# A four-layer graph network on one core: layer entries turned by VectorE and DMAs instead of TensorE, and dense block transposes

## The chip, the core and the metric

The kernel runs on one core of one Trainium2 chip. The core has five engines with an instruction queue each: TensorE (PE; its weight loads stand as PEld), VectorE (DVE), ScalarE (ACT), GpSimd (POOL) and SyncE (SP). SP issues all of this kernel's DMAs. SBUF is the working memory of 128 partitions, PSUM takes what TensorE computes, and DRAM holds inputs, outputs and scratch. The engines run beside each other and are held together by semaphores; each takes its own instructions in the order in which they stand.

The metric is the device time of one execution in microseconds (us), the median over several runs. A profile of one execution shows, in addition, when every instruction started and what it waited for.

## The reference

`x` holds 32 graphs of 512 nodes with 128 features, `adj` is a 512x512 matrix of zeros and ones. Four layers follow each other. Each normalizes x over the features, cuts it at zero, computes something of it and adds that to x:

```python
# before each layer: h = max(layernorm(x), 0);  x = x + layer(h)
# layer 0: attention over adj
x_h  = elu(h @ Wi + bi)
e    = sigmoid(a_tgt[:, :, None] + a_src[:, None, :] + be[0]) * mask(adj)
recv = elu(concat([e @ x_h, x_h * e.sum(-1, keepdims=True)]) @ Wn + bn)
out  = concat([recv, x_h]) @ Wm + bm
# layer 1: a gated step, five times
m  = adj @ h;  av = concat([m, m]);  u3 = h @ u3_w.T + u3_b
z  = sigmoid(av @ w3_w.T + w3_b + u3)
r  = sigmoid(av @ w4_w.T + w4_b + u3)
hv = tanh(av @ w5_w.T + w5_b + (r * h @ u5_w.T + u5_b))
h  = (1 - z) * h + z * hv
# layer 2: adj @ (h @ weight) + bias
# layer 3: h, adj h, adj^2 h, adj^3 h, each times its own 128x128 weight, summed
```

Results are float32.

## The kernel before

**Two layouts.** A graph stands in SBUF either by nodes (a node's number on the partition, four chunks of 128 nodes side by side, each with its 128 features along the row) or by features (a feature on each partition, the 512 nodes along the row). A product with a weight needs the features on the partitions, the product with adj needs the nodes there, and the layernorm needs the nodes there too. So each graph changes its layout at the entry of layers 0, 1 and 3, and after each of the five steps of layer 1.

**From nodes to features** goes over TensorE: `transposed` (L324) makes four 128x128 transposes into a PSUM bank, and `copied` (L350) has ACT copy the bank to SBUF. Layer 0 does this at L457, layer 1 at L696, the entry of layer 3 at L807.

**From features back to nodes** goes over VectorE and two DMAs: `turned` (L333), called at the end of each step of layer 1 (L729). VectorE transposes blocks of 32x32 (L337), and reads its source with a step of four elements while it does. A DMA writes the result to a scratch buffer `m` in DRAM (L340), and a second DMA reads it back in another order of partitions (L342). The result is in nodes, its features in an order that `by_chunk` undoes where ACT and VectorE read it (`parts`, L665, or `add_to_x`, L370).

**Adjacency.** `A_r` holds adj transposed, as float32r. Since adj has only zeros and ones, the branch taken splits the other operand in two float32r parts (`parts`: ACT makes the high one at L672, VectorE the low one at L675) and multiplies in eight passes (`times_adj`, L680). The program holds a second branch for other adjacencies, which doesn't run here.

**The order.** Nothing in the code above issues instructions at once. Each call adds an operation to a plan (`Plan.op`, L53), with its engine, an assumed duration, an assumed time until its result is known (`result`, for DMAs that until landing), a due time, and the buffers it takes. `Plan.order` (L98) then runs through time, and whenever an engine is free gives it, of the operations that are ready, the one with the earliest due time. What comes out is a fixed order for every engine; on the chip each engine follows it and waits where data is late. 32 graphs pass through in groups of four (G = 4), with several graphs in different layers at the same time; due times are spaced by PACE = 56 us for each graph.

**Buffers.** The kinds that matter here are `f` (36 tiles of 128x512 float32 in SBUF), `m` (8 scratch tiles in DRAM), `b` (the 8 banks of PSUM), and `d` (4 rows of DRAM).

**The gather.** For each graph from the fifth on, layer 0 brings a column of scores into a row by two DMAs: `d<-s` (L488) writes 512 single numbers to DRAM, and `f<-d` (L502) reads the row back to all partitions.

Of the kernel before, what the change touches and what calls it, by code (L numbers as in the profile page):

```python
# [16 lines left out]
P = 128  # L17
# [21 lines left out]
class Plan:  # L39
# [13 lines left out]
    def op(self, eng, us, due, emit, reads=(), writes=(), two=False, keep=0, result=None):  # L53

        o = Op(eng, us, self.RESULT[eng] if result is None else result, emit, two, keep)
        for v in reads:
            o.before.add(v.writer)  # L60
        for v in writes:
            o.before.update(v.readers)
            if v.writer:
                o.before.add(v.writer)
            elif v.kind and v.slot is None:
                o.takes.append(v)
        for v in reads:
            v.readers.append(o)
        for v in writes:
            v.writer, v.readers = o, []  # L70
        o.vals = [v.whole or v for v in dict.fromkeys([*reads, *writes])]
        for v in o.vals:
            v.left += 1
        for v in [*reads, *writes, *o.vals]:
            self.vals[v] = True
        o.before -= {o, None}
        o.due = max([due, *(b.due for b in o.before)])
        for b in o.before:
            b.after.append(o)
        self.ops.append(o)  # L80
# [100 lines left out]
def tile_four_graph_layers(  # L181
# [27 lines left out]
    nc = tc.nc  # L209
    B, N, D = x.shape  # L210
    NC = N // P
    G = 4
# [7 lines left out]
    T_MM, T_TR, T_NARROW, T_PASS = 0.86, 0.44, 0.224, 0.23  # L220
    T_VEC, T_COPY, T_ACT = 0.61, 0.5, 0.6
# [3 lines left out]
    op = plan.op  # L225
# [19 lines left out]
    def at(v):  # L245
        if v.tile is not None:
            return v.tile
        return places[v.kind][v.slot] if v.whole is None else at(v.whole)[:, v.part]
# [28 lines left out]
    def load_const(src, shape, name, due, us=0.5):  # L277
        return load(const(name, shape), src, due, us)

    def load_column(src, name, due):  # L280
        return load_const(src.rearrange("(p o) -> p o", o=1), [P, 1], name, due, 0.4)
# [13 lines left out]
    Wi_sb = load_const(Wi, [P, P], "Wi_sb", -9)  # L295
# [3 lines left out]
    bi_sb = load_column(bi, "bi_sb", -8)  # L299
# [20 lines left out]
    bi_half, bn_half = scaled(bi_sb, 0.5, "bi_half", 6), scaled(bn_sb, 0.5, "bn_half", 8)  # L320
# [3 lines left out]
    def transposed(src, due):  # L324

        pt = Val("b")
        def emit():
            for c in range(NC):
                nc.tensor.transpose(at(pt)[:, ts(c, P)], at(src)[:, ts(c, P)], at(ident))  # L329
        op("PE", T_TR, due, emit, [src, ident], [pt])  # L330
        return pt

    def turned(src, due):  # L333


        blocks, moved, t = Val("f"), Val("m"), Val("f")
        op("DVE", 1.03, due, lambda: nc.vector.transpose(  # L337
            at(blocks).rearrange("p (q c f) -> p q c f", c=NC, f=32),
            at(src).rearrange("p (c i q) -> p q c i", c=NC, q=4)), [src], [blocks])
        op("SP", 1.0, due, lambda: nc.sync.dma_start(at(moved), at(blocks)),  # L340
           [blocks], [moved], result=4.0)
        op("SP", 1.0, due, lambda: nc.sync.dma_start(  # L342
            at(t).rearrange("p (b e) -> p b e", e=P),
            at(moved).rearrange("(b i) (q e) -> (i q) b e", i=32, e=P)), [moved], [t], result=6.0)
        return t

    def by_chunk(t):
        return t.rearrange("p (b c f) -> p c b f", c=NC, f=32)

    def copied(src, due, us=T_COPY):  # L350
        t = Val("f")
        op("ACT", us, due, lambda: nc.scalar.copy(at(t), at(src)), [src], [t])  # L352
        return t

    def product(w, src, due, dst=None, start=True, stop=True):
        dst = dst or Val("b")
        op("PE", T_MM, due, lambda: nc.tensor.matmul(  # L357
            at(dst), at(w), at(src), start=start, stop=stop), [src, w], [dst])
        return dst

    def tanh(dst, src, due, bias, scale=0.5, us=T_ACT):
# [50 lines left out]
    for jc in range(NC):  # L412
        pt, z, odd = Val("b"), Val("f"), Val("f")
# [26 lines left out]
    def elu(p, bias, half, due, keep, scale=1.0):  # L440


        e, t, r = Val("f"), Val("f"), Val("f")
        op("ACT", T_ACT, due, lambda: nc.scalar.activation(
            at(e), at(p), AF.Exp, bias=at(bias), scale=scale), [p, bias], [e], keep=keep)
        tanh(t, p, due, half, scale / 2)
        op("ACT", T_ACT, due, lambda: nc.scalar.activation(
            at(r), at(p), AF.Relu, bias=at(bias), scale=scale), [p, bias], [r])
        op("DVE", T_VEC, due, lambda: nc.vector.scalar_tensor_tensor(
            at(t), at(e), 1.0, at(t), op0=ALU.add, op1=ALU.mult), [e, t], [t], two=True)  # L450
        op("DVE", T_VEC, due, lambda: nc.vector.scalar_tensor_tensor(
            at(r), at(t), 0.0, at(r), op0=ALU.min, op1=ALU.add), [t, r], [r], two=True)
        return r

    def layer0(b, h, due):
        KEEP = 12
        hT = copied(transposed(h, due), due)  # L457
        d = due + 6
        xhT = elu(product(Wi_sb, hT, d), bi_sb, bi_half, d, KEEP)

        d = due + 14
        msg, ends = Val("f"), Val("s")
        for half in range(2):
            pt = Val("b")
# [19 lines left out]
        d = due + 20  # L484
# [20 lines left out]
        for jc in range(NC):  # L505
            e = Val("f")
# [15 lines left out]
        d = due + 30  # L522
# [24 lines left out]
        d = due + 44  # L547
# [41 lines left out]
    def list_rest(exact, pool):  # L589
# [41 lines left out]
        for half in range(2):  # L631
            t, outs = Val("f"), slice(half * P // 2, (half + 1) * P // 2)
            load(t, l3_w[:, outs, :].rearrange("i o k -> i (o k)"), 110, 1.3,
                 to=lambda t: t[:, : P // 2 * K])
# [12 lines left out]
        if exact:  # L647
            adjT = A_r
        else:
            adjT = Val(tile=pool.tile([P, NC, N], F32, tag="AT", name="AT"))  # L650
# [3 lines left out]
            for jc in range(NC):  # L654
                pt = Val("b")
# [21 lines left out]
                [src, hi], [lo], two=two)  # L677
            return [lo, hi]

        def times_adj(tok, due):  # L680

            pa = Val("b")
            def emit():
                for jc in range(NC):
                    for n, part in enumerate(tok):
                        nc.tensor.matmul(  # L686
                            at(pa), at(part)[:, ts(jc, P)], at(adjT)[:, jc, :],
                            start=jc == n == 0, stop=jc == NC - 1 and n == PARTS - 1,
                        )
            op("PE", NC * PARTS * T_ADJ, due, emit, [*tok, adjT], [pa])  # L690
            return pa


        def layer1(b, h, due, pace):
            tok = parts(h, due, two=True)
            h = copied(transposed(h, due), due)  # L696
            for t in range(STEPS):
                d = due + t * pace
                u = copied(product(u3T, h, d), d)
                m = copied(times_adj(tok, d), d)  # L700

                def gate(wT, bias, d, m=m, u=u):
                    pg, s = product(wT, m, d), Val("f")
                    op("DVE", T_VEC, d, lambda: nc.vector.tensor_tensor(  # L704
                        at(s), at(u), at(pg), op=ALU.add), [u, pg], [s])
                    tanh(s, s, d, bias)
                    return s

                d += 3
                rh = gate(w4T, w4b, d)  # L710
                op("DVE", T_VEC, d, lambda rh=rh, h=h: nc.vector.scalar_tensor_tensor(  # L711
                    at(rh), at(rh), 1.0, at(h), op0=ALU.add, op1=ALU.mult),
                    [rh, h], [rh], two=True)
                z = gate(w3T, w3b, d + 1)
                d += 4
                pc = product(w5T, m, d, stop=False)
                product(u5T, rh, d, pc, start=False)
                c = Val("f")
                tanh(c, pc, d, w5b, 1.0)

                op("DVE", T_VEC, d, lambda c=c, h=h: nc.vector.tensor_tensor(  # L721
                    at(c), at(c), at(h), op=ALU.subtract), [c, h], [c], two=True)
                op("DVE", T_VEC, d, lambda c=c, z=z: nc.vector.scalar_tensor_tensor(  # L723
                    at(c), at(z), 1.0, at(c), op0=ALU.add, op1=ALU.mult), [z, c], [c], two=True)
                op("DVE", T_VEC, d, lambda c=c, h=h: nc.vector.scalar_tensor_tensor(
                    at(c), at(c), 0.5, at(h), op0=ALU.mult, op1=ALU.add), [c, h], [c], two=True)
                h = c
                d += 5
                h_tok = turned(h, d)  # L729
                if t + 1 < STEPS:  # L730
                    tok = parts(h_tok, d + 9, True, by_chunk)
                else:
                    add_to_x(b, h_tok, d + 9, by_chunk, True)
# [61 lines left out]
        for g in range(NG):  # L795
            bs = range(g * G, (g + 1) * G)
            hT = []
            for b in bs:
# [3 lines left out]
                t = begin(b) + (2.0 if G <= b < B - G - 1 else 1.2) * PACE  # L802
# [49 lines left out]
```

## Time and profile before

| | us |
|---|---|
| median of three runs (1743.92 to 1748.58) | 1746.67 |
| the profiled execution | 1748.12 |
| its span, first to last instruction | 1746.3 |
| mean clock granted to TensorE, of full speed | 0.994 |

The costliest groups that the change touches or stands beside, from the profile (line, operation, count, busy time, mean of one):

| group | count | busy us | mean ns |
|---|---|---|---|
| L686 matmul with adj, 128x512, float32r (layers 1 and 2) | 1536 | 427.6 | 421 |
| L357 matmuls with layer 1's weights, five of them | 1600 | 818.1 | 592 to 599 |
| L329 transposes on TensorE | 384 | 57.6 | 277 |
| L352 copies PSUM to SBUF on ACT | 448 | 256.5 | 588 |
| L337 block transposes on VectorE | 160 | 176.5 | 1105 |
| L704 adds of the gates on VectorE | 320 | 213.6 | 679 |

To read it: a group is all instructions of one line, engine, operation and shape. An fp32 matmul of 512 columns shows as two records, so L357 has 1600 for 800 products. [...] the next begins before it ends, so its mean isn't what the stream of matmuls advances by. Idle time of an engine before a group is named with what ended it. The time of a DMA is counted from its issue on SP to its landing.

### The profile page before, as it was taken

How to read it: one execution, taken by the hardware profiler on the slowest of the kernel's cores; microseconds unless marked ns; L12 is line 12 of the kernel's file. 1: busy time of each engine (PE TensorE's matmuls, PEld its weight loads, DVE VectorE, ACT ScalarE, POOL GpSimd, SP SyncE). 2: the span in 40 equal slices, each digit the busy share in tenths (PEclk: the TensorE clock that was granted, in tenths of full speed). 3: DMA queues.
4: the chain of work that ended last, by engine and by line, in shares of the span. 5: the costliest groups of instructions: out<-in, count | busy, mean ns of one | idle time of the engine just before them, and what ended most of it. 6: DMA issues, size and time to landing. Idle time of an engine off the chain costs nothing.

```text
span 1746.3 us, 21006 instructions
## 1 busy us (share of the span) xinstructions
PE 1695.5 (97%) x6829; PEld 1098.0 (63%) x6829; DVE 1479.3 (85%) x3213; ACT 1135.2 (65%) x2155; POOL 399.8 (23%) x312
## 2 busy tenths in 40 slices
PE   5899999999999999999999999999999999999998
PEld 3555555566666666665666666666666656656797
DVE  6899999999898887888888898888899879878752
ACT  6767765778666666665765667666768656655451
POOL 4521210332222211222212221122232212001110
PEclk9999999999999999999999999999999999999999
DMA  4022322322222222223221221222322131221201
GB/s 109 7 53 75 85 73 73 81 52 85 52 58 61 79 67 46 74 75 55 67 55 60 79 61 61 67 52 81 67 67 55 50 84 61 73 72 58 76 13 48
DMA packets 164534, 112.07 MB, mean 64 GB/s; under 512 B 23232, under 2 KB 139840, under 8 KB 164416
## 3 DMA queue, kind: packets, MB, share of 16 engines
q1 hardware_dynamic: 164416, 110.65, 23.9%
q8 instruction: 55, 0.90, 0.3%
q14 instruction: 63, 0.52, 0.2%
HBM read 60.23 MB, written 50.39 MB: 63 GB/s over the span
## 4 chain that ended last, share of the span: by engine, by line
PE 76%; DVE 13%; DMA 4%; ACT 3%; issue 2%; SPq 0%; DVEq 0%; ACTq 0%
PE b L357 33%; PE b L686 17%; PE b L769 9%; PE b L760 6%; DMA f<-m 4%; PE b L525 4%; PE b L552 3%; DVE f L510 2%; PE b L329 2%; DVE f L704 2%; PE b L743 2%; PE b L469 1%; DVE f L337 1%; DVE f L723 1%; DVE r L675 1%
## 5 line engine op out<-in xcount | busy, mean ns | idle before, releaser
L686 PE MATMUL b<-A_r,r 128*128 128x512 f32 x1536 | 427.6, 421 | 4.3 <-DVE r L675 4.2
L352 ACT COPY f<-b 128x512 f32<-128x512 f32 x448 | 256.5, 588 | 210.6 <-PE b L686 119.2
L686 PEld LDWEIGHTS b<-A_r,r 128*128 128x128 f32 x1536 | 287.2, 189 | 109.6 <-issue 38.9
L391 POOL TENSOR_TENSOR s<-s,nhalf 128x4 f32<-128x4 f32 x128 | 156.2, 1221 | 735.9 <-DVE s L389 707.8
L769 PE MATMUL b<-r,A_r 128*128 128x512 f32 x768 | 306.3, 499 | 0.0
L704 DVE TENSOR_TENSOR f<-f,b 128x512 f32<-128x512 f32 x320 | 213.6, 679 | 56.5 <-PE b L357 54.0
L399 ACT ACTIVATE f<-x,s 128x128 f32<-128x128 f32 x512 | 209.9, 488 | 22.3 <-DVE s L394 22.2
L769 PEld LDWEIGHTS b<-r,A_r 128*128 128x128 f32 x768 | 140.6, 189 | 102.6 <-issue 91.5
L516 POOL TENSOR_TENSOR f<-f,f 128x512 f32<-128x512 f32 x96 | 154.1, 1608 | 207.4 <-DVE f L510 131.1
L362 ACT ACTIVATE f<-f,b4w 128x512 f32<-128x512 f32 x160 | 115.8, 724 | 127.3 <-DVE f L704 126.6
L337 DVE STREAM_TRANSPOSE f<-f 128x512 f32<-128x512 f32 x160 | 176.5, 1105 | 0.3
L675 DVE TENSOR_TENSOR r<-f,r 128x512 fp32r<-128x512 f32 x192 | 141.3, 739 | 37.1 <-ACT r L672 37.0
L357 PE MATMUL b<-f,u5T 128*128 128x512 f32 x320 | 163.2, 595 | 8.7 <-DVE f L711 8.7
L357 PE MATMUL b<-f,w4T 128*128 128x512 f32 x320 | 165.2, 599 | 4.1 <-ACT f L352 4.0
L357 PE MATMUL b<-f,w3T 128*128 128x512 f32 x320 | 163.8, 594 | 0.0
L357 PE MATMUL b<-f,w5T 128*128 128x512 f32 x320 | 163.2, 595 | 0.0
L357 PE MATMUL b<-f,u3T 128*128 128x512 f32 x320 | 162.7, 592 | 0.0
L721 DVE TENSOR_TENSOR f<-f,f 128x512 f32<-128x512 f32 x160 | 121.5, 761 | 39.3 <-ACT f L362 39.1
L760 PEld LDWEIGHTS b<-V,f 128*128 128x128 f32 x1024 | 131.7, 191 | 31.1 <-issue 25.1
L362 ACT ACTIVATE f<-b,b5w 128x512 f32<-128x512 f32 x160 | 109.7, 688 | 60.4 <-PE b L357 60.2
L362 ACT ACTIVATE f<-f,b3w 128x512 f32<-128x512 f32 x160 | 115.0, 721 | 50.8 <-DVE f L704 50.5
L525 PE MATMUL b<-f,f 128*128 128x512 f32 x256 | 130.9, 596 | 3.2 <-issue 3.0
(95 smaller groups left out, 2489.9 us busy)
## 6 DMA issues: line engine op xcount, KB each, us to landing
m<-f SPq DMA_DIRECT2D x160, 256.0 KB, 2.0
f<-m SPq DMA_DIRECT2D x160, 256.0 KB, 2.8
x<-in_x_dram SPq DMA_DIRECT2D x32, 256.0 KB, 4.5
out_dram<-x SPq DMA_DIRECT2D x32, 256.0 KB, 2.4
f<-d SPq DMA_DIRECT2D x28, 256.0 KB, 4.1
f<-in_adj_dram SPq DMA_DIRECT2D x4, 256.0 KB, 4.6
f<-in_L_gnn_weight_dram SPq DMA_DIRECT2D x2, 224.0 KB, 2.6
d<-s SPq DMA_DIRECT2D x28, 2.0 KB, 9.1
```

Of the source, the lines that this page charges most:

```text
L337: op("DVE", 1.03, due, lambda: nc.vector.transpose(at(blocks).rearrange("p (q c f) -> p q c f", c=NC, f=32), at(src).rearrange("p (c i q) ...
L352: op("ACT", us, due, lambda: nc.scalar.copy(at(t), at(src)), [src], [t])
L357: op("PE", T_MM, due, lambda: nc.tensor.matmul(at(dst), at(w), at(src), start=start, stop=stop), [src, w], [dst])
L362: op("ACT", us, due, lambda: nc.scalar.activation(at(dst), at(src), AF.Tanh, bias=at(bias), scale=scale), [src, bias], [dst])
L391: op("POOL", 1.2, due, lambda: nc.gpsimd.tensor_tensor(stat(SCALE), stat(VAR), at(neg_half), op=ALU.pow), [s, neg_half], [s])
L399: nc.scalar.activation(at(h)[:, ts(c, P)], at(X[b])[:, c, :], AF.Relu, bias=stat(SHIFT)[:, c : c + 1], scale=stat(SCALE)[:, c : c + 1],)
L525: op("PE", T_MM, d, lambda jc=jc: nc.tensor.matmul(at(pn), at(msg)[:, ts(jc, P)], at(es[jc]), start=jc == 0, stop=False), [msg, es[jc]], [pn])
L675: op("DVE", T_VEC, due, lambda: nc.vector.tensor_tensor(part(lo), whole(), part(hi).bitcast(F32), op=ALU.subtract), [src, hi], [lo], two=two)
L686: nc.tensor.matmul(at(pa), at(part)[:, ts(jc, P)], at(adjT)[:, jc, :], start=jc == n == 0, stop=jc == NC - 1 and n == PARTS - 1,)
L704: op("DVE", T_VEC, d, lambda: nc.vector.tensor_tensor(at(s), at(u), at(pg), op=ALU.add), [u, pg], [s])
L760: nc.tensor.matmul(at(pz)[:, ts(i, D)], at(hT[i])[:, ts(ic, P)], at(V[k]), start=i == 0, stop=last and i == G - 1,)
L769: nc.tensor.matmul(at(pz), at(adjT)[:, jc, ts(ic, P)], at(part), start=False, stop=jc == NC - 1 and n == PARTS - 1,)
```

## The change

It has three parts.

1. `turned` transposes densely: VectorE reads and writes whole rows in order. The write to scratch is as before. [...] the second DMA becomes four, each of 32 partitions. The plan's assumptions change with it: 0.63 us for VectorE (1.03 before), 3.0 us until the write has landed (4.0), 1.6 us for the four issues (1.0 for one), 4.0 us until they have landed (6.0).
2. Since the block transposes are dense, layer 1 keeps its columns in block order: the row of a feature holds, for each of the four quarters of a chunk, the 32 nodes of each chunk. `times_adj` reads adj's columns in that order in layer 1 (`by_block`: 16 runs of 32 elements). Products with weights, gates and sums don't see the order.
3. A new function `turned_back` goes from nodes to features without TensorE: a block transpose on VectorE, four DMAs to scratch, one DMA back. Layer 0 uses it for the graphs from the fifth on (28), layer 1 from the ninth on (24); the first graphs keep TensorE's transposes, with layer 1's copy on ACT putting the columns in block order. In layer 0 the product with Wi reads the block order and writes its PSUM bank in the usual one. Where it is used, the due times of what follows are 8 us later.

```diff
     def turned(src, due):
         blocks, moved, t = Val("f"), Val("m"), Val("f")
-        op("DVE", 1.03, due, lambda: nc.vector.transpose(
-            at(blocks).rearrange("p (q c f) -> p q c f", c=NC, f=32),
-            at(src).rearrange("p (c i q) -> p q c i", c=NC, q=4)), [src], [blocks])
+        op("DVE", 0.63, due, lambda: nc.vector.transpose(at(blocks), at(src)), [src], [blocks])
         op("SP", 1.0, due, lambda: nc.sync.dma_start(at(moved), at(blocks)),
-           [blocks], [moved], result=4.0)
-        op("SP", 1.0, due, lambda: nc.sync.dma_start(
-            at(t).rearrange("p (b e) -> p b e", e=P),
-            at(moved).rearrange("(b i) (q e) -> (i q) b e", i=32, e=P)), [moved], [t], result=6.0)
+           [blocks], [moved], result=3.0)
+        def carry():
+            for q in range(4):
+                nc.sync.dma_start(
+                    at(t)[ts(q, 32), :].rearrange("p (b e) -> p b e", e=P),
+                    at(moved)[:, ts(q, P)].rearrange("(b i) e -> i b e", i=32),
+                )
+        op("SP", 1.6, due, carry, [moved], [t], result=4.0)
         return t
+
+    def turned_back(src, due):
+        blocks, moved, t = Val("f"), Val("m"), Val("f")
+        op("DVE", 0.63, due, lambda: nc.vector.transpose(
+            at(blocks).rearrange("p (b c i) -> p b c i", c=NC, i=32),
+            at(src).rearrange("p (c b f) -> p b c f", c=NC, f=32)), [src], [blocks])
+        def carry():
+            for q in range(4):
+                nc.sync.dma_start(
+                    at(moved)[:, ts(q, P)].rearrange("(b f) e -> f b e", f=32),
+                    at(blocks)[ts(q, 32), :].rearrange("p (b e) -> p b e", e=P),
+                )
+        op("SP", 1.6, due, carry, [blocks], [moved], result=3.0)
+        op("SP", 1.0, due, lambda: nc.sync.dma_start(at(t), at(moved)),
+           [moved], [t], result=4.0)
+        return t
+
+    def by_block(t):
+        return t.rearrange("p (c q i) -> p q c i", c=NC, i=32)
...
-    def product(w, src, due, dst=None, start=True, stop=True):
+    def product(w, src, due, dst=None, start=True, stop=True, view=None):
         dst = dst or Val("b")
-        op("PE", T_MM, due, lambda: nc.tensor.matmul(
-            at(dst), at(w), at(src), start=start, stop=stop), [src, w], [dst])
+        def emit():
+            to = at(dst) if view is None else view(at(dst))
+            of = at(src) if view is None else at(src).rearrange("p (q c i) -> p q c i", c=NC, i=32)
+            nc.tensor.matmul(to, at(w), of, start=start, stop=stop)
+        op("PE", T_MM, due, emit, [src, w], [dst])
         return dst
...
     def layer0(b, h, due):
         KEEP = 12
-        hT = copied(transposed(h, due), due)
+        if b < G:
+            hT = copied(transposed(h, due), due)
+        else:
+            hT = turned_back(h, due)
+            due += 8
         d = due + 6
-        xhT = elu(product(Wi_sb, hT, d), bi_sb, bi_half, d, KEEP)
+        xhT = elu(product(Wi_sb, hT, d, view=by_block if b >= G else None),
+                  bi_sb, bi_half, d, KEEP)
...
-        def times_adj(tok, due):
+        def times_adj(tok, due, view=lambda t: t):
...
-                            at(pa), at(part)[:, ts(jc, P)], at(adjT)[:, jc, :],
+                            at(pa), at(part)[:, ts(jc, P)], view(at(adjT)[:, jc, :]),
...
         def layer1(b, h, due, pace):
             tok = parts(h, due, two=True)
-            h = copied(transposed(h, due), due)
+            if b < 2 * G:
+                pt, h = transposed(h, due), Val("f")
+                op("ACT", T_COPY, due, lambda h=h, pt=pt: nc.scalar.copy(
+                    at(h).rearrange("p (q c i) -> p q c i", c=NC, i=32), by_block(at(pt))),
+                    [pt], [h])
+            else:
+                h = turned_back(h, due)
+                due += 8
             for t in range(STEPS):
                 d = due + t * pace
                 u = copied(product(u3T, h, d), d)
-                m = copied(times_adj(tok, d), d)
+                m = copied(times_adj(tok, d, by_block), d)
```

## The prediction

> **What bounds the kernel now.** I read the page's busy shares first, then the busy time of the long middle stretch, then the pace of TensorE in the chain of waits.
>
> ```profile
> PE 1695.5 (97%) x6829; PEld 1098.0 (63%) x6829; DVE 1479.3 (85%) x3213; ACT 1135.2 (65%) x2155; POOL 399.8 (23%) x312
> ...
> PE 76%; DVE 13%; DMA 4%; ACT 3%; issue 2%; SPq 0%; DVEq 0%; ACTq 0%
> ...
> 100.00:1600.00 1500.00, 1478.02 (x5740) 936.41 (x5739) 1320.23 (x2800) 1002.00 (x1888) 329.27 (x240) 1.00 0.25 66
> ```
>
> PE is busy 97% of the span and 1478 of the 1500 us from 100 to 1600 us, at full clock. Ends of matmuls are modelled, so I check the pace. The chain and the timeline hold unbroken runs:
>
> ```profile
> 131.94 6.87 PE b L357 x16
> ...
> 139.68 3.65 PE b L686 x16
> ...
> 1691.38 5.36 PE b L760 x48
> ...
> 387.82 0.49 PE L329 MATMUL b<-ident,f 128*128 128x128 f32 x3
> ```
>
> One record of an fp32 matmul over 512 columns takes 6.87/16 = 0.429 us (two records a matmul), one of float32r 3.65/16 = 0.228, one 128 wide 5.36/48 = 0.112. Three transposes last 0.49 us, the last of them 0.273 (its own duration in the trace), so one costs the stream (0.49 - 0.273)/2 = 0.109. With the counts of the groups: 1992 x 0.4285 + 2360 x 0.228 + 2048 x 0.111 + 421 x 0.109 = 1665 us. That is what PE needs with no stall. The span is 1746.3, so 81 us are stalls: from the start times of the matmuls 30 lie in the first 100 us, 43 between 100 and 1640 us, 8 at the end. In most stretches of 50 us PE loses 0.2 to 0.3 us: this kernel is bound by PE's stream, and anything taken off PE counts whole unless it comes back as a stall.
>
> **Where the 43 us come from.** The views by line of the DMA issues, and the timeline around 304 us:
>
> ```profile
> m<-f SPq DMA_DIRECT2D x160, 256.0 KB, 2.0
> f<-m SPq DMA_DIRECT2D x160, 256.0 KB, 2.8
> d<-s SPq DMA_DIRECT2D x28, 2.0 KB, 9.1
> ...
> DMA to landing us min/median/max: 2.5/2.8/12.2
> ...
> 303.59 0.37 SPq L488 DMA_DIRECT2D d<-s  x1
> 304.07 0.45 SPq L342 DMA_DIRECT2D f<-m  x1
> 304.56 0.51 SPq L290 DMA_DIRECT2D x<-in_x_dram  x1
> ...
> 315.77 0.62 ACT L672 CAST r<-f 128x512 fp32r<-128x512 f32 x1 [3.53 <-DMA f<-m]
> ...
> 317.17 2.99 PE L686 MATMUL b<-A_r,r 128*128 128x512 f32 x8 [2.11 <-DVE r L675]
> ...
> ACT r L672 <- DMA f<-m: 23.0, 8, 3.7
> ```
>
> The gather d<-s (2 KB in 4-byte pieces, once for each of 28 graphs) takes 9 us, and every DMA issued behind it lands only some 12 us after its issue. A read f<-m that follows it takes 11.5 to 12.2 us instead of 2.8 (fourth line: its longest). ACT waits 3.5 us for it and PE 2.1 us after that. This happened 8 times, 23 us of ACT waits. PE's loss in the 20 us after the gathers sums to 19 us; the other 24 us stand mostly before u5T products that wait for DVE.
>
> [...]
>
> **The change part by part.**
>
> *Entries off PE.* Layer 0 of 28 graphs and layer 1 of 24 lose four transposes each: 52 x 4 x 0.109 = 22.7 us of PE stream. ACT loses the copy behind them: 52, and 8 remain under another line, so 52 x 0.588 = 30.6 us on an engine at 65%; worth nothing by itself.
>
> *VectorE.* A dense transpose: [...] the add of L704 shows 679[...] I take 0.69. Turns save 160 x (1.105 - 0.69) = 66 us, entries add 52 x 0.69 = 36 [...]. Net -30 of 1479. It relieves the waits for u5T; I take 8 of the 24 us, bounds 0 and 15.
>
> *Matmuls over strided columns.* 1280 float32r matmuls read adjT in 16 runs of 128 bytes. [...] I take 0; the upper bound, one lost cycle a run, an estimate of 16 x 0.43 ns (from 0.228 us for 512 columns, 0.45 ns each) x 1280 = 9 us. The 28 Wi products write PSUM in runs of 32: 28 x 0.86 = 24 us in all, taken as unchanged, +5 at most.
>
> *The queue.* A turn goes from 2 DMAs to 5, an entry adds 5: SP issues 160 x 3 + 52 x 5 = 740 more, beside some 460 now. Issues follow each other at 0.48 us (303.59, 304.07, 304.56), so SP's issuing rises by 355 us; it has room for that, but a read now has its last quarter issued 1.5 us after its first, so 4.3 us to landing instead of 2.8. In the program's order of instructions SP also waits, before each DMA, for the one eight places earlier (eight completion semaphores in turn): eight places are now 1.6 turns, not four.
>
> *The planner's margins.* The order on every engine is fixed by the plan, and its costs changed. A turn, from VectorE's start to the landing, was planned at 1.03+0.5+1+4+1+6 = 13.5 us and takes 1.1+2.0+2.8 = 5.9; it becomes 0.63+0.5+1+3+1.6+4 = 10.7 planned and 0.69+2.0+4.3 = 7.0 real. The margin shrinks from 7.6 to 3.7 us. That cover is what hides most gathers now. In PE's order the work that stands between a turn's last product and the matmuls that use it shrinks too: counted from the order with the durations above, median 29.7 to 27.8 us, least 21.3 to 19.2.
>
> *The sum.* In SP's order the first turn DMA behind a gather is a read in 11 of 28 cases before and in 15 after, a write in 7 and in 9 (the rest are entries or loads). Before, the 11 reads cost 19 us, 1.7 each; behind a write nothing was lost. After, a read's plan ends 1.4 us earlier (5.6 against 7.0), its fourth piece is the last in line, and ACT's wait passes to PE nearly one to one: 1.7 + 1.4 to 2.4, so 15 x 3.1 to 4.1 = 46 to 61 us. A turn whose write hits was planned at 12 us for both DMAs, now 9.6, and takes longer (two transfers, 10 + 4.3): about 1.5 us late at PE, 9 x 1.5 = 13 us. Middle: 53 + 13 = 66 against 19, +47; but two hits behind one gather share a stall, so I take +41 (bounds +10, if the cushions of PE's order hold, and +60). Entries behind a gather: their products are for graphs not due yet, 0.
>
> 1746.3 - 22.7 - 8 + 41 = 1756.6 us span; the profiled execution took 1748.1 with its start and end, and the median of the runs is 1746.7, on the span. Forecast 1757.
>
> **Rivals.**
> - *The saving holds (faster, 1726).* One mechanism: the cushion in PE's order, 19 us of work at least against some 12 us of real turn. Seven of the eleven reads behind gathers cost PE nothing before; if a lateness of 1.5 us more stays inside that cushion, stalls stay near 19 us and 1746.7 - 22.7 + 2 = 1726. It decides at an extra gather stall of 22.7 + 8 = 31 us, about 1.2 us a gather. For it: PE's pace, which leaves nothing else to lose. Against: where ACT waited for the DMA, PE waited too.
> - *Balance (1746).* Extra stalls of 25 to 36 us, the lower end of my estimate: within 5 us of now, so within 0.3%, about what a measurement of this kernel can tell from no change.
> - *TensorE or SP pays (slower, 1770).* The strided reads cost 10% (1280 x 23 ns = 29 us), with half of the stalls: 1746.7 - 30.7 + 20 + 29 = 1765, or SP becomes late in bursts of twelve issues (12 x 0.48 = 5.8 us), which adds the 3.7 us margin to some ten turns: 1757 + 20 = 1777. [...] SP's waits of 859 us for DVE (it is mostly idle) against the second.
> - *It does not do what it says:* not possible for the transposes; the order of PE has 104 of 6951 rows less over both branches, and the count agrees.
>
> **Numbers.** My forecast 0.47 (own range 1750 to 1775), the saving holds 0.31, balance 0.13, TensorE or SP 0.09. Slower by over 0.3% 0.57, within 0.3% 0.12, faster 0.31. The range reaches to 1724 on the side of the rival and to 1780: 2 in 10 outside.
>
> **What would show it.** Right: PE's transposes 176 instead of 384 records at L329; the dense transpose near 0.69 us; ACT's wait for f<-m well over 23 us; PE's stalls after gathers two to three times 19 us. Wrong: waits of ACT for DMAs at 23 us or less with PE at the same pace, then 1726; or the spacing of float32r records in layer 1 above 0.228, then the third rival.

## The result, and the profile after

The changed kernel takes 1766.55 us (median of 4 runs) against 1746.46 us before (4 runs): a ratio of 1.0117, 95% interval 1.0095 to 1.0139. It is slower. Its profiled execution has a span of 1764.2 us, 17.9 more than before.

The page of the changed kernel, busy shares, chain and two groups:

```profile
PE 1691.9 (96%) x6621; PEld 1083.7 (61%) x6621; DVE 1449.3 (82%) x3265; ACT 1110.0 (63%) x2103; POOL 400.4 (23%) x312
...
PE 69%; DVE 13%; DMA 10%; ACT 4%; issue 2%; SPq 1%; DVEq 0%; ACTq 0%
...
L704 ACT CAST r<-f 128x512 fp32r<-128x512 f32 x192 | 118.0, 620 | 74.7 <-DMA f<-m 66.4
...
f<-m SPq DMA_DIRECT2D x640, 64.0 KB, 2.0
f<-m SPq DMA_DIRECT2D x52, 256.0 KB, 2.8
```

PE has 208 matmul records fewer (6829 to 6621, the transposes), but its busy time hardly falls and its share does: the work went, the time didn't. In the chain DMA went from 4% to 10%. The cast on ACT (L704, once L672) was idle before it for 23.2 us; now for 74.7, of which 66.4 wait for reads f<-m.

The reads by line, L343, in the changed kernel:

```profile
DMA to landing us min/median/max: 1.7/2.0/11.3
```

And its timeline from 807 us (start, duration, engine, instruction; in brackets the idle time before it and what ended it):

```profile
807.05 0.37 SPq L520 DMA_DIRECT2D d<-s  x1
807.52 1.87 SPq L343 DMA_DIRECT2D f<-m  x4
...
819.11 0.62 ACT L704 CAST r<-f 128x512 fp32r<-128x512 f32 x1 [4.95 <-DMA f<-m]
...
816.92 1.02 PE L384 MATMUL b<-f,u3T 128*128 128x512 f32 x2
821.80 2.07 PE L384 MATMUL b<-f,w4T 128*128 128x512 f32 x2 [3.85 <-ACT f L376]
```

A quarter of a read lands 2.0 us after its issue in the middle, and 11.3 at worst. The timeline is the picture of before at 304 us, deeper: a gather, four reads right behind it, ACT waits 4.95 us for the last of them, and PE then stands for 3.85 us, because the copy it needs is queued on ACT behind that cast.

PE's stalls, worked out as in the prediction (time between matmul starts less the pace of 0.4285, 0.228, 0.111 or 0.109 us a record):

| us of PE | before | after |
|---|---|---|
| stream without stalls | 1665.8 | 1643.1 |
| stalls to 100 us | 24.1 | 30.1 |
| stalls from 100 to 1640 us, within 4 to 24 us of a gather's issue | 19.0 | 55.6 |
| stalls from 100 to 1640 us, elsewhere | 23.7 | 22.8 |

The stream is counts times pace, so its fall says only that 208 records went. By this account 22.7 us of stream were saved and 36.6 given back behind gathers; 6 more came in the first 100 us.

Not all of a stall is standing. The two lines of PE above show it: two records take 1.02 us before the stall of 3.85 us and 2.07 after it. The stretch before 821 us and the one behind it (length, busy time of each engine, then the clock granted to TensorE, third from the end):

```profile
814.00:821.00 7.00, 3.95 (x24) 2.90 (x22) 1.24 (x3) 2.05 (x6) 0.04 (x1) 1.00 0.05 12
821.00:827.80 6.80, 6.00 (x8) 2.80 (x9) 6.80 (x16) 2.95 (x6) 0.00 (x0) 0.50 0.41 136
```

From 100 to 1640 us the trace has seven such stretches at half the clock, 3.4 or 6.8 us long, 30.7 us in all; before it has four, 13.7 us. Each lies at a stall of about 2 us or more, though not every such stall has one. Matmuls that start in them cost some 13 us more than their pace, before 6; these are part of the 78.4 and 42.7 us of stalls between 100 and 1640 us.

### The profile page after: what moved, and what is told of

Same layout as the page of the kernel before. It is cut to its first block, busy times and chain, and to the rows that moved or that the text cites. A ratio compares the mean times of both kernels' runs of the same rounds, so it can differ in the third digit from the quotient of the medians.

```text
span 1764.2 us, 22081 instructions
## 1 busy us (share of the span) xinstructions
PE 1691.9 (96%) x6621; PEld 1083.7 (61%) x6621; DVE 1449.3 (82%) x3265; ACT 1110.0 (63%) x2103; POOL 400.4 (23%) x312
## 4 chain that ended last, share of the span: by engine, by line
PE 69%; DVE 13%; DMA 10%; ACT 4%; issue 2%; SPq 1%; DVEq 0%; ACTq 0%
PE b L384 31%; PE b L718 14%; PE b L808 8%; DMA f<-m 8%; PE b L799 5%; PE b L557 4%; PE b L584 2%; DVE f L542 2%; DMA m<-f 1%; DVE f L743 1%; PE b L782 1%; DVE r L707 1%; PE b L501 1%; DVE s L413 1%; SPq L343 1%
## 5 line engine op out<-in xcount | busy, mean ns | idle before, releaser
L718 PE MATMUL b<-A_r,r 128*128 128x512 f32 x1536 | 434.3, 425 | 2.6 <-DVE r L707 2.6
L376 ACT COPY f<-b 128x512 f32<-128x512 f32 x388 | 223.2, 586 | 191.8 <-PE b L718 119.7
L808 PE MATMUL b<-r,A_r 128*128 128x512 f32 x768 | 321.3, 518 | 0.0
L707 DVE TENSOR_TENSOR r<-f,r 128x512 fp32r<-128x512 f32 x192 | 136.0, 713 | 71.6 <-ACT r L704 60.4
L704 ACT CAST r<-f 128x512 fp32r<-128x512 f32 x192 | 118.0, 620 | 74.7 <-DMA f<-m 66.4
L760 DVE TENSOR_TENSOR f<-f,f 128x512 f32<-128x512 f32 x160 | 116.5, 730 | 29.4 <-ACT f L389 29.1
```

The costliest lines, as they stand in the source:

```text
L707: op("DVE", T_VEC, due, lambda: nc.vector.tensor_tensor(part(lo), whole(), part(hi).bitcast(F32), op=ALU.subtract), [src, hi], [lo], two=two)
L718: nc.tensor.matmul(at(pa), at(part)[:, ts(jc, P)], view(at(adjT)[:, jc, :]), start=jc == n == 0, stop=jc == NC - 1 and n == PARTS - 1,)
L808: nc.tensor.matmul(at(pz), at(adjT)[:, jc, ts(ic, P)], at(part), start=False, stop=jc == NC - 1 and n == PARTS - 1,)
```

## The experiments

Theory A: the plan's shorter assumed times place a turn's consumers closer to their DMAs, so that a DMA held up by a gather, once covered, now stops ACT and then PE. Theory B: the additional DMAs themselves (four reads for one, SP's longer queue) make the turns late. Theory C, beside A: the loss comes from standing behind the gather in SP's queue. The kernel before took 1746 us beside the changed kernel, 1754 beside e1 to e4 and 1759 to 1760 beside the others (e1 to e4 ran on one chip, e5 and e8 to e10 on a second, the rest on a third; why the times differ stays open). So each ratio is to runs of the kernel before that were taken beside it; its stalls and waits are those of its one profile, of 1748 us, and are compared less closely. "Behind gathers" is, as above, what begins within 4 to 24 us of a gather's issue.

| kernel | ratio to before | 95% interval | PE stalls, 100 to 1640 us | of these behind gathers | ACT's cast waits for f<-m, us (times) |
|---|---|---|---|---|---|
| before | 1 | | 42.7 | 19.0 | 23.0 (8) |
| changed | 1.0117 | 1.0095 to 1.0139 | 78.4 | 55.6 | 66.4 (20) |
| e1: changed, assumed times as before | 0.9915 | 0.9899 to 0.9932 | 51.7 | 30.6 | 48.4 (16) |
| e2: before, short assumed times | 1.0106 | 1.0089 to 1.0122 | 70.2 | 52.8 | 57.2 (11) |
| e3: changed, gather from ACT's queue | 0.9876 | 0.9859 to 0.9892 | 52.7 | 35.4 | 51.3 (20) |
| e4: before, gather from ACT's queue | 0.9870 | 0.9852 to 0.9887 | 25.0 | 10.5 | 4.7 (5) |
| e5: before, reads in four | 0.9994 | 0.9981 to 1.0007 | 49.8 | 28.4 | 31.4 (10) |
| e8: changed, no gather | 0.9725 | 0.9709 to 0.9741 | 15.4 | no gather | 0.5 (1) |
| e9: before, no gather | 0.9855 | 0.9838 to 0.9871 | 16.3 | no gather | none listed |
| e10: e1, no gather | 0.9768 | 0.9752 to 0.9784 | 21.6 | no gather | none listed |
| f1: e2, no gather | 0.9844 | 0.9828 to 0.9861 | 14.3 | no gather | none listed |
| f2: changed, entries left on TensorE | 1.0022 | 1.0011 to 1.0033 | 60.7 | 49.1 | 65.5 (21) |
| f3: before, layer 0's entries alone | 0.9919 | 0.9903 to 0.9936 | 51.6 | 31.4 | 57.5 (20) |
| g1: changed, turns' assumed times as before | 0.9966 | 0.9952 to 0.9979 | 59.9 | 33.0 | 35.9 (16) |

In g1 one stall of 8.8 us begins 3.6 us behind a gather and is counted in.

One reading crosses the table. Where the turns have the short assumed times, 49 to 56 us are lost behind gathers (changed, e2, f2); where they have the long ones, 19 to 33 (before, e1, e5, f3, g1), whatever else is changed while SP issues the gather.

### The assumed times: e1 and e2

e1, in both `turned` and `turned_back`:

```diff
-           [blocks], [moved], result=3.0)
+           [blocks], [moved], result=4.0)
...
-        op("SP", 1.6, due, carry, [moved], [t], result=4.0)
+        op("SP", 1.6, due, carry, [moved], [t], result=6.0)
```

> The changed kernel, with the plan's assumed times until landing as before (4.0 and 6.0 us, in both functions); nothing else. Theory A (the shorter assumed times place consumers too close to their DMAs, and the stalls behind the gather grew from 19 to 56 us of PE): the waits of ACT's cast for f<-m fall from 66 to below 35 us, time 1730 to 1745. Theory B (the four-fold reads themselves and SP's longer queue make DMAs late, whatever the plan assumes): time stays at 1757 to 1768, the waits above 50 us.

e2, in `turned` of the kernel before:

```diff
-           [blocks], [moved], result=4.0)
+           [blocks], [moved], result=3.0)
...
-            at(moved).rearrange("(b i) (q e) -> (i q) b e", i=32, e=P)), [moved], [t], result=6.0)
+            at(moved).rearrange("(b i) (q e) -> (i q) b e", i=32, e=P)), [moved], [t], result=4.0)
```

> The kernel before, with the changed kernel's assumed times (3.0 and 4.0 us in place of 4.0 and 6.0); one read a turn as before. Theory A: slower, 1760 to 1780, and ACT's waits for f<-m go from 23 to over 50 us. Theory B: same, 1744 to 1751.

No matmul and no DMA is added or taken away in either; only the order changes. The longer times take the changed kernel from 1.0117 to 0.9915, faster than before; the shorter ones take the kernel before to 1.0106, with none of the change's other parts: behind gathers they cost 33.8 us of PE where the whole change cost 36.6. Theory B expected no movement in either. Nor do fewer reads meet a gather: in e1 a turn's read is issued within 1.1 us behind 14 of the 28 gathers, in the changed kernel behind 11, in e2 behind 10 and before behind 8. The waits, by e1 and by e2:

```profile
ACT r L704 <- DMA f<-m: 48.4, 16, 4.3
```

```profile
ACT r L672 <- DMA f<-m: 57.2, 11, 9.1
```

The longest single wait (last column) is 9.1 us in e2 and 4.3 in e1; it was 3.7 before. In e1 the waits in all fell less than theory A expected (48.4, not below 35), but PE's stalls fell from 78.4 to 51.7: the shorter waits reach PE less. What an arbitrary new order costs by itself was not measured; without gathers the same two changes of order moved the time by 0.1 and 0.4% (below).

### Are four reads dearer than one: e5

```diff
+        def carry():
+            for k in range(4):
+                nc.sync.dma_start(
+                    at(t)[ts(k, 32), :].rearrange("p (b e) -> p b e", e=P),
+                    at(moved).rearrange("(b i) (q e) -> (i q) b e", i=32, e=P)[ts(k, 32)],
+                )
+        op("SP", 1.6, due, carry, [moved], [t], result=6.0)
```

> The kernel before with each read f<-m cut in four of 32 partitions (assumed 1.6 us for the issues, 6.0 until landing, as before; write unchanged). Theory A (margins): the real turn gets some 0.7 us longer and its planned one 0.6 us, so within 0.5% of before: 1744 to 1755. Theory B (four DMAs for one, SP's queue and its eight completion semaphores make turns late): slower by 10 us or more.

They cost nothing that can be measured (0.9994): 480 more DMAs on SP's queue, with the assumed times kept long, leave the time where it was. (The forecast of 1744 to 1755 us was missed: the kernel before itself took 1759 us beside e5's 1758.6.) Theory B falls for the reads.

### The gather in another queue: e3 and e4

```diff
-                nc.sync.dma_start(
+                nc.scalar.dma_start(
                     at(row).rearrange("o (c p) -> p (o c)", c=NC), at(ends)[:, NC : 2 * NC]
...
-            op("SP", 0.6, due + 10, gather, [ends], [row], result=11.0)
+            op("ACT", 0.1, due + 10, gather, [ends], [row], result=11.0)
```

> The changed kernel with the 28 gathers d<-s issued from ACT's queue in place of SP's. Theory C (the loss comes from DMAs that stand behind a gather in SP's queue): the longest landing of f<-m falls from 11.3 us to below 6, ACT's waits for it to under 15 us, time 1705 to 1725. If DMAs of another queue are held up just as much, or if the lost time has nothing to do with the gathers: 1755 to 1770.

> The kernel before with the 28 gathers issued from ACT's queue. Theory C: PE's stalls behind gathers, 19 us, go: 1725 to 1735; the difference to the changed kernel with the same edit is then the change's own worth without gathers, about 20 us. Rival: unchanged, 1744 to 1751.

Both got faster, but not for the reason of theory C. e4 lies in its range with 1730 us; e3 missed what theory C gave on every count with 1733 us, waits of 51.3 us and a longest landing of 11.4, and the two differ by 3 us, not 20. The timeline of e3 from 696 us:

```profile
696.34 2.38 SPq L343 DMA_DIRECT2D f<-m  x3
...
697.89 0.38 ACTq L520 DMA_DIRECT2D d<-s  x1
...
709.06 1.14 ACT L704 CAST r<-f 128x512 fp32r<-128x512 f32 x2 [4.68 <-DMA f<-m]
```

And e3's reads by line:

```profile
DMA to landing us min/median/max: 1.7/2.0/11.4
```

The gather is in ACT's queue now, and the reads in SP's still take up to 11.4 us; of the three that start at 696.34 the last was issued at 698.3, just behind the gather, and landed 10.7 us later. A gather holds up the DMAs of the other queue as well. What fell is the number of gathers with a read issued within 1.1 us behind them: in e4 three, in the kernel before eight; in e3 seven, in the changed kernel eleven. That this is because SP no longer waits for the scores before it can issue what stands behind the gather, is argued from the order of SP and was not tried apart; the edit also gives the whole plan another order.

### No gather: e8, e9, e10 and f1

```diff
-        if b < G:
+        if True:
             tgt = Val("b")
             op("PE", T_TR, d, spread, [ends, ident], [tgt])
```

> The changed kernel with the scores spread by four TensorE transposes for all graphs, as it does for the first four: no gather and no f<-d, 28 x 4 x 0.109 = 12 us more of PE stream. If the gathers are what the short margins run into: PE's 56 us of stalls go, f<-m never takes longer than 6 us, time 1764 - 56 + 12 = 1720, range 1712 to 1732. If the short margins cost as much at other DMAs: above 1745.

> The kernel before with the same edit. 1746 - 19 + 12 = 1739, range 1732 to 1746. The difference to the changed kernel with this edit is the change's worth without gathers: 18 to 23 us if the PE stream alone decides.

> The changed kernel with the assumed times of before and no gather. Without gathers the margins should matter little: within 6 us of the changed kernel with no gather. If longer margins help by 10 us or more there too, DMAs other than those behind gathers come late.

> The kernel before with the short assumed times (3.0 and 4.0 us) and no gather. The short times alone cost 1.9% more than the old ones could hide when gathers were there (ratio 1.0106 to before). If they hurt only through gathers: ratio 0.978 to 0.987, no slower than the old times without a gather (0.9855). If they hurt by themselves: 0.990 or more.

This adds four transposes for each of 28 graphs, 12.2 us of stream, and takes the gather away. With it go f<-d and SP's waits for the scores and for the gather's landing, so these runs don't part the hold-up of other DMAs from what else comes with a gather. The busy time in the stretch from 100 to 1600 us, of e8 and then of e9 (the stretch and its length, then PE, its weight loads, VectorE, ACT, POOL, the clock and DMA):

```profile
100.00:1600.00 1500.00, 1498.73 (x5786) 947.08 (x5784) 1308.97 (x2915) 999.42 (x1880) 318.77 (x244) 1.00 0.27 81
```

```profile
100.00:1600.00 1500.00, 1495.00 (x5907) 953.47 (x5905) 1314.38 (x2823) 1016.82 (x1917) 327.22 (x240) 1.00 0.19 62
```

The landing of their reads, e8 and e9:

```profile
DMA to landing us min/median/max: 1.8/2.0/3.9
```

```profile
DMA to landing us min/median/max: 2.5/2.8/4.0
```

PE is busy 1498.7 and 1495.0 of the 1500 us, where the changed kernel has 1456.3. None of these reads takes more than 4.0 us. e8 took 1711.5 us, just under its range, and e9 1733.7, in its range: without gathers the change is worth 22 us, a ratio of 0.987, which agrees with the 22.7 us of stream that it takes off PE. And the short assumed times cost nothing there: f1 against e9 0.9844 to 0.9855 (each to its own runs of before), e8 against e10 1711.5 to 1719.0 us, so the long ones then even cost 7.6 us, where at most 6 were expected. (The 1.9% in the text on f1 is 1.1% by the ratio that stands beside it.) The short times hurt only where there are gathers.

e8 beats both kernels: 2.75% under the kernel before.

### Which part needs the margin: f2, f3, g1

f2 leaves every entry on TensorE (dense turns, block order and short times stay); f3 puts only layer 0's entries into the kernel before, with the long times; g1 has the long times in `turned` and the short ones in `turned_back`:

```diff
-        if b < G:
+        if True:
             hT = copied(transposed(h, due), due)
...
-            if b < 2 * G:
+            if True:
                 pt, h = transposed(h, due), Val("f")
```

> The changed kernel with all entries of layers 0 and 1 left on TensorE: dense turns, block order in layer 1 and the short assumed times alone. PE's stream is as long as before (1665 us), so theory A gives before plus the stalls that the short times add, some 30 to 37 us with 4 us for the strided reads of adj: ratio 1.012 to 1.025. If the entries' extra DMAs are what makes the turns late, not the turns' own assumed times: 0.997 to 1.006.

> The kernel before with only layer 0's entries of 28 graphs turned by VectorE and DMAs (assumed 4.0 and 6.0 us); turns as before. PE's stream is 28 x 4 x 0.109 = 12.2 us shorter: ratio 0.991 to 0.996 if it costs nothing else; 0.998 or more if the entries' own DMAs and VectorE's extra work take the gain back.

> The changed kernel with the longer assumed times (4.0 and 6.0 us) in the turns alone; the entries keep the short ones (3.0 and 4.0). If the turns' own assumed times carry the loss: ratio to before 0.989 to 0.996, as with both longer. If the entries' assumed times carry it: 1.005 to 1.015, as with both short. In between if each has a share.

f3 came as the stream says: 0.9919, 13 us between the medians for 12.2 expected. f2 missed: 1.0022 where theory A gave at least 1.012. Its waits are those of the changed kernel:

```profile
ACT r L704 <- DMA f<-m: 65.5, 21, 7.1
```

yet PE's stalls are 60.7 us, 18 over those of the profiled kernel before, not 30. The part behind gathers did come as theory A gave it, 49.1 us, 30 more than before. Elsewhere the stalls are 11.6 us, 12 fewer, of which 7 stood before u5T products that wait for VectorE (9.3 before, 2.0 in f2; 11.8 in the changed kernel). VectorE has the dense transposes there without the entries' work, which would explain it; that was not tried apart. And the kernel before ran 13 us slower beside f2 than beside the changed kernel and was not profiled there, so its own stalls may have been larger.

g1 stands between, as forecast if each has a share: of the step from 1.0117 to 0.9915, the turns' assumed times carry (1.0117 - 0.9966) / (1.0117 - 0.9915) = three quarters, across different chips. Behind gathers they carry nearly all: 33.0 us in g1, 30.6 in e1, 55.6 in the changed kernel. What g1 loses against e1 lies mostly away from gathers (26.9 us against 21.1) and in the first 100 us (33.2 against 29.4), and why stays open.

## Why the prediction was right, point by point

It forecast 1757 us, slower, by a margin lost behind gathers; measured were 1766.55. That the shorter assumed times carry the loss, and only where there are gathers, is shown by e1, e2, e8 and f1. All four signs that the prediction named for being right came: 176 records at L329, a dense transpose near 0.69 us, ACT's waits at 66.4 us, stalls behind gathers at 2.9 times 19 us.

- *PE's stream, -22.7 us:* 208 records went, as counted. That they are worth it on the chip is shown by e8 against e9, 22 us.
- *Stalls behind gathers, 19 to 60 us:* measured 19.0 to 55.6. The estimate of the rise, +41, was +36.6. The picture of what hits holds too: of ACT's 66.4 us of waits for reads, 57 us belong to 13 reads whose last quarter was issued within 3.5 us behind a gather. "Nearly one to one" from ACT to PE does not hold everywhere: f3 has 57.5 us of waits and 31.4 of stalls behind gathers. And the price of a stall in the forecast was taken whole from before; that a part of it is matmuls at half the clock was not seen.
- *VectorE, 0.69 us a transpose:* 701 ns at L338 and 702 at L353; busy time fell by 30.0 us, as forecast. (The 0.69 us was the author's estimate, beside an addition of the same size that takes 679 ns in the trace; no dense transpose had been measured. The transposes came within 4% of the addition.) Its worth for PE, 8 us, was too high: stalls away from gathers fell by 0.9, and by some 5 with the next point taken out. Those before u5T products, which it was to relieve, were 9.3 of the 24 us, not most, and became 11.8.
- *Strided columns, taken as 0, at most 9 us:* in the changed kernel the median step between the starts of matmuls is 234 ns in layer 1, which reads 16 runs of 32, and 231 in layer 2, which reads 512 in one run (mean 233.8 and 230.5 of those under 250 ns). 1280 x 3.2 = 4.1 us. The 0 was the author's estimate; the term was mis-sized, not missed. The sign for the third rival, a step above 228 ns, was set too low: before, the same line steps by 231.
- *The queue:* a quarter lands 2.0 us after its issue, so a read takes 3 x 0.47 + 2.0 = 3.4 us, not 4.3. The wait for the DMA eight places earlier is in the trace of the changed kernel: the completion semaphores of its 1208 issues go round eight without an exception, and of 1200 issues none began before the DMA eight places earlier had landed, where 55 began before the one seven places earlier had. Four issues in place of one were not seen to cost anything (e5, ratio 0.9994); in the changed kernel one issue of a read, behind the gather at 863 us, took 6.6 us, and what such a case costs was not taken apart.
- *The first 100 us:* not in the sum; 6 us of stalls came there. In the profile the granted clock of that stretch is 0.90 where it was 0.97; 3 of the 6 us are matmuls at half the clock. Why it was half for longer is open.

Together, in spans: 1764.2 against 1756.6 forecast, 7.6 us. Stalls away from gathers were 7.1 us over the forecast (-0.9 for -8, 4.1 of it the columns), the start 6.0 over, the gathers 4.4 under, and the two ends were 1 us shorter. So part of the nearness is luck: the loss behind gathers was put 4.4 us too high where the rest of the sum was some 13 us too low. The median of the runs stands 2.3 us above this span.

- *The rival in which the saving holds* is what happens without gathers (e8 and e9); with them the cushion of PE's order did not hold.
- *"Every DMA issued behind it"* was too narrow and too wide: in e3, with the gather in ACT's queue, reads of SP's queue took up to 11.4 us, against 11.3 in the changed kernel. Nor does every DMA behind a gather take some 12 us: those issued 2 to 4 us behind it in the changed kernel took 7.4 to 11.7.
- *Two sums* are not what they say: the third rival's 20 us would be ten turns at 5.8 - 3.7 = 2.1 us, where ten at 3.7 are 37; and 0.228 us for 512 columns is 0.45 ns each, not 0.43, which makes the bound 9.2 us.

## What to carry to other kernels

Where a plan fixes the order, an assumed latency is a margin against what a transfer takes behind its slowest neighbour, and not only against its median. Here 10 us assumed for the two DMAs of a turn lost 19 to 33 us behind gathers and 7 us lost 49 to 56; where that neighbour was gone, the shorter times cost nothing. Look for one small DMA in tiny pieces before trimming margins; here 28 gathers of 2 KB decided whether the same change won 1.3% or lost 1.2%. A saving on the engine that bounds a kernel counts whole only while nothing that feeds it comes late: 22.7 us less of PE's stream were worth 22 us without gathers, and with them the time rose by 20.

## What the runs showed of the hardware that was not expected

- A DMA of 512 single 4-byte numbers, which itself took 8.1 to 11.0 us in the changed kernel, held up reads issued behind it from the same queue and from another engine's: reads of SP's queue landed up to 11.3 us after their issue with the gather in SP's queue too (the changed kernel) and up to 11.4 with the gather in ACT's (e3), where the median is 2.0 in both; without gathers none of a turn's reads took over 4.0 us (e8 and e9).
- Behind some stalls of PE of 2 to 4 us the granted clock was half for 3.4 or 6.8 us, and matmuls took 1.87 to 1.99 times their pace in the median of a stretch: seven times between 100 and 1640 us in the changed kernel, four times before. The mean granted clock of the whole profiled execution was 0.985 in the changed kernel and 0.994 in e8.
- A dense VectorE transpose of 128x512 fp32 took 701 ns (the changed kernel, L338), one that reads with a step of 16 bytes 1105 (before, L337).
- Reading the moving operand in runs of 128 bytes cost a float32r matmul of 512 columns 3 ns in 231 (the changed kernel, layer 1 against layer 2).
- In the median a read of 64 KB landed 2.0 us after its issue and one of 256 KB 2.8 us; the four issues that replace one followed each other on SP at 0.47 us in the changed kernel, and in e5 four for one cost nothing that can be measured (0.9994).
